# A plan of 2640 words in another order, and each attention's second result copy on ScalarE

## The chip, the cores and the metric

The kernel runs on one core of one Trainium2 chip. The metric is the device time of one execution in microseconds (us). The kernel before takes 887.47 us, the median of three runs (886.60, 887.47, 888.52).

The engines are called as the profile calls them: PE is TensorE, DVE is VectorE, ACT is ScalarE, POOL is GpSimd, and SP issues transfers. Each works through its own instructions in the order of the program and waits on semaphores for the results of the others.

## The reference

Sixteen batches of 256 tokens by 256 features, in float32, go through a cross attention with RMS norms (layer 0), and then through a block with a causal self attention (layer 1), a cross attention (layer 2) and a feed-forward part with 1024 hidden features. There are 16 heads of 16 features everywhere.

```python
# layer 0
q_norm, c_norm = rmsnorm(query, g_q), rmsnorm(context, g_c)
Q, K, V = heads(q_norm @ Wq), heads(c_norm @ Wk), heads(c_norm @ Wv)
attn = softmax(Q @ K.T * hd ** -0.5)             # the mask is all ones
x = rmsnorm(query + merge(attn @ V) @ Wo, g_out)
# layer 1: causal, queries and keys turned by their position (rope)
h = ln(x); x = x + attn_causal(rope(h @ wq), rope(h @ wk), h @ wv) @ wo
# layer 2: queries from x, keys and values from the context y, rope on both
h = ln(x); x = x + attn(rope(h @ wq), rope(y @ wk), y @ wv) @ wo
x = x + gelu(ln(x) @ fc1 + b1) @ fc2 + b2
```

## The kernel before, in words

**The work.** There are 48 attentions, one for each batch and layer. `ORDER` fixes which layer the i-th attention has (the string begins 000001010102); a batch's attention of layer 1 follows its layer 0, and layer 2 follows layer 1. After the 48 attentions the feed-forward parts of all batches run two batches at a time (`Mlp`); this last part, from about 680 us on, is written out as code and not touched by the plan but for its first steps.

**The plan.** Between a short head and that last part, all instructions come from the string `PLAN` (L54). Its words, such as `scores.6.1` or `take_last.5`, name a step and an attention. `step` (L1507) holds one Python generator per word: the first time a word appears it runs up to the first `yield`, the next time up to the second, and so on. So a word that stands four times has four parts, each issuing its instructions where the word stands. Since nothing reorders instructions later, the place of a word is its place in the queue of each engine that it uses, SP's and POOL's queues of transfers included. The words are grouped in the text by attention: a line begins with `scores.i.0`.

**The steps of one attention**, in the order in which one attention needs them:
- `stats`, `norm`: row statistics on DVE (L543), the inverse root on POOL (L525, L526), the normalized rows `xn` on DVE (L553). `keep` (L729, L620) then adds the output bias to the rows on POOL (L621, 128x512).
- `pieces`: DVE transposes 32x32 blocks into the tile `bits` (L584), and its second part sends it to DRAM (SP, L592). `pieces_in` fetches the turned rows `hT` (SP, L598). `turn` does the same through PE and ACT instead.
- `q`, `k`, `v`: a projection is 32 matmuls into one of three PSUM tiles `d` (L633 or L645). In layers 1 and 2, ACT adds the bias (L760) into a tile `a`; DVE turns by position (shuffle L768, two products L774, an addition L863, L866 or L810). The tag `a` has two buffers, and `bits` and `qa` use them too.
- `q_high`, `q_low`, `q_out`, `k_high`, `k_low`, `k_out` (layers 0 and 2, from the third attention on): a split in a high and a low part on ACT (L823, L875) and DVE (L830, L834, L879), and transfers on SP that put the parts on the rows where the matmuls need them (L840, L887). Layer 1 instead writes two masked copies of the query (L816 on DVE, L818 on ACT).
- `scores.i.n`: one block of scores, 16 matmuls (L953 in layer 1, L964 otherwise) into two PSUM tiles `S`, of which there are just two; then two exponentials on ACT (L976) into tiles `pt`. In layer 1, POOL clears what lies above the diagonal (L984).
- `values.i.n`: 8 matmuls for each block (L1007) into the PSUM tile `A`, of which there is one. After the first half of the features is done, the second part of `values.i.1` copies `A` to SBUF on ACT (`take(0, ...)`, L1022). After the second half, `take_last` (L1034) copies it; before, this copy is on DVE.
- `sums_in` (L1041) and `heads_in` (L1030): SP moves the softmax sums and the heads from the copied tile `av` to where they are needed. Both wait for the copies.
- `invert`: a reciprocal on DVE (L1051), out to DRAM and back over all rows (L1054, L1060). `divide`: a check sum on POOL (L1065), and the product on DVE (L1067).
- `project`: 32 matmuls (L645) and the addition to the rows on DVE (L1074 or L1080); `finish` (L1084) ends layer 0.

**Other words.** `load_piece`, `load_later` issue input and weight loads on POOL's queue, `load_early` and `load` on SP's. `send`, `receive` carry a row scale through DRAM. `combine` (L1480) does one of eight POOL operations (L1124, L1135) that prepare sums of the feed-forward weights; before, the first four calls prepare the second weight matrix and the last four the first one, whatever number the word has.

Of the kernel before, what the change touches and what calls it, by code (L numbers as in the profile page):

```python
# [54 lines left out]
scores.0.0 scores.0.0 v.0 scores.0.0 scores.0.1 q.1 scores.0.1 scores.0.1 spread.1 spread.1  # L55
scores.0.2 q.1 v.1 v.1 v.0 scores.0.2 v.0 scores.0.2 stats_x.3 values.0.0 values.0.1 stats_x.2
stats_x.3 scores.0.3 v.1 values.0.1 load_piece.5.0 k.1 stats_x.2 scores.0.3 send.2 stats_y.2
scores.0.3 k.2 send.2 k.1 load_piece.5.1
scores.1.0 load_early.4 k_high.2 load_early.0 k_low.2 q.2 scores.1.0 send.3 receive.2 scores.1.0
values.0.2 load_early.3 send.3 scores.1.1 q.3 scores.1.1 q.2 scores.1.1 values.0.3 k_out.2  # L60
q_high.2 scores.1.2 take_last.0 q_low.2 v.2 v.2 stats_y.2 scores.1.2 receive.3 q_low.2 stats_y.3
scores.1.2 q_out.2 values.1.0 stats_y.6 load_piece.6.1 scores.1.3 sums_in.0 stats_y.3 stats_x.6
k.3 scores.1.3 scores.1.3 load.4 values.1.1 k_high.3
scores.2.0 values.1.1 k_low.3 scores.2.0 values.1.2 q.3 invert.0 values.1.3 scores.2.0 heads_in.0
take_last.1 q_high.3 scores.2.1 invert.0 v.3 k_out.3 q_low.3 scores.2.1 q_low.3 heads_in.0
scores.2.1 v.2 stats_x.4 q_out.3 scores.2.2 k.4 stats_x.4 stats_y.4 sums_in.1 scores.2.2
load_piece.5.2 send.4 scores.2.2 values.2.0 v.3 send.4 divide.0 v.3 k_high.4 scores.2.3 q.4
load_early.2 scores.2.3 invert.0 invert.1 k_low.4 scores.2.3 divide.1 values.2.1 stats_y.4
receive.4 invert.1
scores.3.0 heads_in.1 values.2.1 stats_x.6 fold_of_att scores.3.0 heads_in.1 load_piece.5.3  # L70
values.2.2 divide.0 scores.3.0 q.4 values.2.3 k_out.4 q_high.4 scores.3.1 take_last.2 project.0
q_low.4 scores.3.1 invert.1 q_low.4 scores.3.1 values.3.0 q_out.4 project.0 fold_of_att scores.3.2
project.0 v.4 v.4 load_piece.6.0 scores.3.2 stats_y.8 project.0 scores.3.2 values.3.1 sums_in.2
finish.0 scores.3.3 values.3.1 stats.5 k.6 fold_of_att scores.3.3 v.4 stats.5 scores.3.3
values.3.2 load_later.0 norm.5 k_high.6 divide.1 load_piece.6.2
scores.4.0 heads_in.2 stats_x.8 values.3.3 scores.4.0 turn.5 send.6 send.6 take_last.3 scores.4.0
project.1 fold_of_att fold_of_att turn.5 heads_in.2 k_low.6 scores.4.1 invert.2 project.1 q.5
sums_in.3 scores.4.1 fold_of_att load_early.1 scores.4.1 receive.6 values.4.0 project.1 heads_in.3
q.5 scores.4.2 invert.3 k.5 project.1 invert.2 q.5 scores.4.2 q.5 load_later.1 invert.3 scores.4.2
q.5 values.4.1 load_piece.7.1 q.5 k.5 load_piece.7.0 scores.4.3 q.5 invert.2 values.4.1  # L80
load_piece.7.2 q.6 k.5 q.5 stats_y.6 k.5 scores.4.3 k.5 heads_in.3 v.5 v.5 scores.4.3 divide.2 k.5
load_piece.6.3 q.6 stats_x.8 values.4.2 invert.3 v.5 q_high.6
scores.5.0 divide.3 finish.1 q_low.6 k_out.6 values.4.3 scores.5.0 v.6 take_last.4 scores.5.0
scores.5.0 stats.7 sums_in.4 scores.5.1 divide.2 stats.7 q_low.6 project.2 v.6 scores.5.1 norm.7
scores.5.0 pieces.7 q_out.6 scores.5.1 scores.5.1 values.5.0 project.2 pieces.7 scores.5.2
project.2 scores.5.1 heads_in.4 k.8 send.8 invert.4 scores.5.2 project.2 divide.3 invert.4
scores.5.2 v.6 scores.5.2 values.5.1 finish.2 keep.5 k_high.8
scores.6.0 values.5.1 stats.9 pieces_in.7 project.3 scores.6.0 scores.5.2 k_low.8 stats.9
scores.6.0 values.5.2 heads_in.4 divide.4 norm.9 stats_y.8 project.3 scores.6.1 take_last.5
load_later.9 q.7 scores.6.1 project.3 sums_in.5 load_later.8 scores.6.1 pieces.9 heads_in.5  # L90
values.6.0 stats_y.10 q.7 scores.6.2 pieces.9 k.7 q.7 send.8 scores.6.2 invert.5 q.7 invert.5
scores.6.2 invert.4 q.7 values.6.1 q.7 scores.6.3 receive.8 q.7 k.7 q.8 invert.5 q.7 k.7
values.6.1 pieces_in.9 v.7 v.7 k.7 scores.6.3 load_later.4 k.7 load_piece.7.3 scores.6.3 k.7
heads_in.5 values.6.2 divide.5 q.8 project.3
scores.7.0 divide.4 q_high.8 v.7 k_out.8 project.4 scores.7.0 stats_x.10 scores.7.0 scores.7.0
values.6.3 heads_in.6 load_later.5 scores.7.1 divide.5 scores.7.0 take_last.6 project.5 project.4
scores.7.1 q_low.8 scores.7.1 scores.7.1 q_low.8 v.8 project.5 q_out.8 scores.7.1 stats.11
scores.7.2 sums_in.6 project.4 stats.11 q.9 scores.7.2 load_later.7 norm.11 scores.7.2 finish.3
scores.7.2 values.7.0 heads_in.6 pieces.11 stats_x.10 q.9 values.7.1
scores.8.0 load_piece.8.0 q.9 values.7.1 k.10 pieces.11 scores.7.2 scores.8.0 q.9 v.8 load_later.6  # L100
scores.8.0 send.10 values.7.2 v.8 send.10 stats_y.10 gain_ca k_high.10 q.9 scores.8.1 project.4
k.9 q.9 scores.8.1 keep.7 pieces_in.11 take_last.7 invert.6 scores.8.1 values.8.0 stats_x.14 k.9
invert.6 scores.8.2 q.9 v.9 v.9 k.9 load_piece.9.0 scores.8.2 k_low.10 divide.6 sums_in.7
load_piece.8.1 scores.8.2 k.9 values.8.1 keep.9 k.9 q.9 scores.8.3 values.8.1 invert.6 k.11 v.9
scores.8.3 k.9 heads_in.7 scores.8.3 finish.4 values.8.2 invert.7 receive.10 k.11 heads_in.7
scores.9.0 k.11 values.8.3 invert.7 scores.9.0 k.11 k_out.10 q.10 take_last.8 scores.9.0
scores.9.0 k.11 load_later.10 sums_in.8 scores.9.1 q.10 scores.9.0 stats.13 stats_x.14 q_high.10
v.10 divide.6 v.10 scores.9.1 divide.7 q_low.10 invert.7 stats.13 project.6 scores.9.1 q_low.10
scores.9.1 v.10 q_out.10 scores.9.2 project.6 scores.9.1 heads_in.8 invert.8 q.11 k.11 scores.9.2
load_piece.8.2 heads_in.8 divide.7 scores.9.2 load_piece.9.1 values.9.0 send.14 project.6  # L110
scores.9.2 q.11 invert.8 values.9.1 scores.9.2 k_high.11
scores.10.0 q.11 load_later.3 values.9.1 project.7 norm.13 scores.10.0 k_low.11 scores.10.0 q.11
values.9.2 k_out.11 pieces.13 q.11 scores.10.1 project.7 k.12 scores.10.1 take_last.9 q.11
scores.10.1 invert.8 values.10.0 stats.12 q_high.11 pieces.13 scores.10.2 stats.12 sums_in.9 v.11
q_low.11 scores.10.2 divide.8 norm.12 load_piece.10.0 k.12 heads_in.9 q_low.11 v.11 turn.12
scores.10.2 k.12 values.10.1 q_out.11 stats.16 turn.12 scores.10.3 pieces_in.13 values.10.1 v.11
fold_of_fc1 stats.16 scores.10.3 divide.8 q.12 load_later.2 k.12 scores.10.3 k.12 load_piece.8.3
k.12 values.10.2 q.12 stats_y.14
scores.11.0 fold_of_fc1 k_high.12 project.8 fold_of_fc1 invert.9 scores.11.0 stats_y.14 norm.16
heads_in.9 q.12 scores.11.0 project.6 values.10.3 k_low.12 invert.9 q.12 scores.11.1 q.12 k_out.12  # L120
k.13 scores.11.1 take_last.10 q.12 scores.11.1 heads_in.10 values.11.0 q_high.12 scores.11.2
invert.9 v.12 v.12 divide.9 q_low.12 scores.11.2 keep.11 send.14 q_low.12 scores.11.2 project.8
values.11.1 q_out.12 gain_fc1.0 k.13 scores.11.3 divide.9 k.14 sums_in.10 scores.11.3 v.12
scores.11.3 project.9 pieces.16 keep.12 values.11.1 k.13 k_high.14
scores.12.0 k.13 project.9 values.11.2 scores.12.0 k.13 pieces.16 values.11.3 heads_in.10 stats.15
scores.12.0 take_last.11 heads_in.11 stats.15 scores.12.1 k.13 q.13 receive.14 norm.15 scores.12.1
sums_in.11 invert.10 scores.12.1 k_low.14 divide.10 values.12.0 project.8 invert.10 q.13
scores.12.2 heads_in.11 q.13 values.12.1 scores.12.2 pieces_in.16 q.13 v.13 v.13 scores.12.2 q.13
q.13 values.12.1 invert.10 scores.12.3 q.13 q.13 pieces.15 q.14 scores.12.3 v.13 pieces.15
scores.12.3 k_out.14 values.12.2 q.14  # L130
scores.13.0 divide.10 fold_of_fc1 finish.6 k.15 scores.13.0 pieces_in.15 stats.19 scores.13.0
stats_x.17 scores.13.0 values.12.3 q_high.14 scores.13.1 take_last.12 k.15 invert.11 v.14 v.14
# [216 lines left out]
def xattn_kernel(  # L349
# [21 lines left out]
    nc = tc.nc  # L371
# [285 lines left out]
    class Att:  # L657
# [376 lines left out]
        def take_last(self, copy=nc.vector.tensor_copy):  # L1034

            self.take(1, copy)
# [459 lines left out]
    def begin(word):  # L1496
# [3 lines left out]
        if name == "combine":  # L1500
            return combine()
# [563 lines left out]
```

## Time and profile before

| | us |
|---|---|
| median of three runs | 887.47 |
| the profiled execution | 891.12 |
| its span | 889.40 |
| PE busy in the span | 871.22 |
| DVE, ACT, POOL busy | 690.87, 570.42, 349.33 |
| PE busy in 20 to 680 us (660 us) | 650.10 |
| copies L1022 on ACT | 49, median 0.587 |
| copies L1022 on DVE | 47, median 0.684 |

The profiled execution is one run with the hardware profiler on; its span reaches from the first to the last instruction. "Busy" is the time in which at least one instruction of that engine ran; the ends of matmuls are modelled, so a busy PE may still be slowed. A row of the windows view gives, for a stretch, the busy time (and instruction count) of PE, the weight loads PEld, DVE, ACT and POOL, then the granted clock of PE as a share of full speed, the share of the transfer engines, and GB/s. A row of the waits view gives who waited, for whom, how long in total, how often, and the longest. In a row of the timeline the two numbers are start and duration, `x2` merges equal neighbours, and the bracket gives the idle time before the first one and what ended it.

### The profile page before, as it was taken

What the parts mean: (1) busy time and instruction counts of PE and PEld (TensorE: products, weight loads), DVE (VectorE), ACT (ScalarE), POOL (GpSimd) and SP (SyncE); (2) the same over time, 40 slices, a digit from 0 to 9 for tenths busy, and PEclk for the clock granted to TensorE, in tenths of its full rate; (3) what the DMA queues carried; (4) which work ended last, traced back from release to release, by engine and by line L of the source; (5) the groups of instructions that cost most, each with busy time, mean ns of one, the idle gap of its engine ahead of it and who ended that gap; (6) DMA issues with size and microseconds to landing.
All of it is one profiled execution on the core that took longest, in us unless ns stands there. A gap on an engine that the chain in (4) does not pass through costs nothing.

```text
span 889.4 us, 32873 instructions
## 1 busy us (share of the span) xinstructions
PE 871.2 (98%) x13762; PEld 559.2 (63%) x13762; DVE 690.9 (78%) x1534; ACT 570.4 (64%) x801; POOL 349.3 (39%) x558
## 2 busy tenths in 40 slices
PE   8999999999999999999999999999999999999997
PEld 4455555555555555555554555555556799999997
DVE  5468789888888889889885888989894677777662
ACT  4787567776686767778756777777875733334440
POOL 3234766517364246175483335345142132221000
PEclk9999999999999999999999999999999999999999
DMA  8666455544444344343434233233431022111201
GB/s 273 208 193 176 147 163 175 178 132 133 134 148 123 110 134 161 117 159 120 155 118 145 84 124 111 87 118 116 158 107 54 17 72 72 57 44 44 72 25 50
DMA packets 101454, 107.04 MB, mean 120 GB/s; under 512 B 26602, under 2 KB 81778, under 8 KB 101298
## 3 DMA queue, kind: packets, MB, share of 16 engines
q1 hardware_dynamic: 96210, 89.89, 30.7%
q0 software_dynamic: 4400, 14.42, 5.7%
q8 instruction: 110, 1.80, 0.9%
q10 hardware_dynamic: 688, 0.54, 0.2%
q14 instruction: 46, 0.38, 0.1%
HBM read 46.33 MB, written 13.65 MB: 67 GB/s over the span
## 4 chain that ended last, share of the span: by engine, by line
PE 79%; DVE 8%; DMA 5%; ACT 2%; issue 2%; SPq 2%; POOL 2%; ACTq 0%; DVEq 0%; POOLq 0%
PE d L633 15%; PE d L645 14%; PE A L1007 14%; PE S L964 7%; PE upX L1221 6%; PE A L1319 6%; PE S L953 5%; PE downZ L1319 3%; PE upZ L1221 3%; PE d L1319 2%; PE d L1221 2%; ACT pt L976 1%; DMA turn_hop<-bits 1%; DMA qm<-qm 1%; DVE xn L553 1%
## 5 line engine op out<-in xcount | busy, mean ns | idle before, releaser
L976 ACT ACTIVATE pt<-S 128x1024 f32<-128x1024 f32 x224 | 217.7, 1023 | 98.9 <-PE S L953 59.4
L1007 PE MATMUL A<-pt,va 128*32 128x256 f32 (+1 forms) x3072 | 184.6, 363 | 2.9 <-ACT av L1022 2.7
L976 ACT ACTIVATE pt<-S,sy 128x1024 f32<-128x1024 f32 x128 | 136.4, 1115 | 35.5 <-PE S L964 26.2
L1007 PEld LDWEIGHTS A<-pt,va 128*32 128x32 f32 x3072 | 94.1, 110 | 68.0 <-issue 7.0
L984 POOL TENSOR_SCALAR_AFFINE_SELECT pt<-pt 128x512 f32<-128x512 f32 x128 | 90.7, 728 | 74.4 <-ACT pt L976 73.9
L964 PEld LDWEIGHTS S<-qm,kT 32*128 32x128 f32 x1920 | 66.9, 183 | 52.2 <-issue 24.2
L964 PE MATMUL S<-qm,kT 32*128 32x256 f32 x1920 | 93.5, 304 | 3.8 <-ACT pt L976 3.4
L621 POOL TENSOR_TENSOR cur<-cur,bias 128x512 f32<-128x512 f32 x48 | 64.8, 1353 | 32.9 <-DVE xn L553 32.7
L525 POOL TENSOR_SCALAR r_ln<-bmv 128x2 f32<-128x2 f32 x48 | 14.4, 300 | 149.6 <-DVE bmv L544 137.4
L953 PE MATMUL S<-qm,kT 32*64 32x512 f32 (+1 forms) x1152 | 63.3, 512 | 1.1 <-DVE kT L866 1.0
L760 ACT ACTIVATE a<-d,qk_bias 128x256 f32<-128x256 f32 x128 | 53.9, 477 | 14.0 <-PE d L633 4.8
L1243 ACT COPY g<-upX 128x512 f32<-128x512 f32 x28 | 15.0, 589 | 72.4 <-issue 68.1
L633 PE MATMUL d<-hT,sa 128*32 128x256 f32 x1024 | 61.4, 382 | 0.0
L553 DVE TENSOR_SCALAR xn<-cur,bmv,r_ln 128x256 f32<-128x256 f32 x96 | 47.5, 543 | 4.2 <-POOL r_ln L526 4.0
L1067 DVE TENSOR_TENSOR oT<-oT,inv 128x512 f32<-128x512 f32 x48 | 38.2, 798 | 15.1 <-DMA rq<-rq_hop 3.7
L774 DVE TENSOR_TENSOR a<-a,turn 128x512 f32<-128x512 f32 x64 | 47.9, 748 | 1.3
L1259 ACT ACTIVATE g<-g,fb 128x256 f32<-128x256 f32 x96 | 41.0, 499 | 11.1 <-DVE g L1248 11.1
L768 DVE STREAM_SHUFFLE u<-a 128x512 f32<-128x512 f32 x64 | 47.5, 743 | 0.4 <-issue 0.4
L774 DVE TENSOR_TENSOR u<-u,turn 128x512 f32<-128x512 f32 x64 | 47.0, 734 | 0.0
L1065 POOL TENSOR_TENSOR seen<-seen,sums 128x64 f32<-128x64 f32 x48 | 20.9, 436 | 62.9 <-DVE sums L1051 59.2
L633 PEld LDWEIGHTS d<-hT,sa 128*32 128x32 f32 x1024 | 30.3, 109 | 24.2 <-issue 3.2
L1022 DVE COPY av<-A 128x512 f32<-128x512 f32 x47 | 32.1, 683 | 13.4 <-PE A L1007 13.4
(176 smaller groups left out, 1701.1 us busy)
## 6 DMA issues: line engine op xcount, KB each, us to landing
kT<-hl SPq DMA_DIRECT2D x60, 256.0 KB
qm<-qm SPq DMA_DIRECT2D x60, 256.0 KB
oT<-av SPq DMA_DIRECT2D x192, 64.0 KB
inv<-inv_hop SPq DMA_DIRECT2D x96, 128.0 KB
turn_hop<-bits SPq DMA_DIRECT2D x33, 256.0 KB
hT<-turn_hop SPq DMA_DIRECT2D x92, 64.0 KB
out<-res SPq DMA_DIRECT2D x15, 256.0 KB
cur<-in_x POOLq DMA_DIRECT2D x11, 256.0 KB, 3.3
```

What stands on the lines that cost most here:

```text
L553: nc.vector.tensor_scalar(xn[:, c, :], src[:, c, :], mv[:, c, 0:1], r[:, c : c + 1], ALU.subtract, ALU.mult,)
L621: nc.gpsimd.tensor_tensor(t, t, bias_sb[:, row : row + D].unsqueeze(1).to_broadcast([P, NC, D]), ALU.add)
L633: nc.tensor.matmul(o, lhsT=w[:, k, at + t * P + j : at + t * P + j + 32], rhs=tokens, start=(k == 0), stop=(k == KC - 1), skip_group_check ...
L645: nc.tensor.matmul(ps[j : j + 32, c * D : (c + 1) * D], lhsT=some_tokens(src, k, c, j), rhs=w[:, k, at : at + D], start=(k == 0), stop=(k ...
L774: nc.vector.tensor_tensor(t, t, table.unsqueeze(1).to_broadcast([P, KC, S]), ALU.mult)
L953: nc.tensor.matmul(ps[64 * half : 64 * half + 64, 2 * m * u : 2 * m * (u + 1)] .rearrange("p (i s) -> p i s", i=2), lhsT=self.kT[r, t, at] ...
L964: nc.tensor.matmul(ps[:, at : at + m], lhsT=self.kd[r, i, t, kc * P : (kc + 1) * P].bitcast(F32R), rhs=self.qd[r, i, h, t, q0:S].bitcast(F ...
L976: nc.scalar.activation(pt[:, :, :w], ps[:, :, :w], AF.Exp, scale=scale)
L984: nc.gpsimd.affine_select(out=diag, in_=diag, compare_op=ALU.is_ge, fill=0.0, base=0, pattern=[[0, 2], [0, 2], [1, P]], channel_multiplier=-1,
L1007: nc.tensor.matmul(self.av[32 * r : 32 * r + 32, i, q0:S], lhsT=self.va[:, kc, 8 * t + 2 * r + i, :], rhs=pts[r // 2][:, r % 2, i * m : (i ...
L1221: nc.tensor.matmul(o if len(b.shape) == 2 else by_groups(o), lhsT=a[:, c * P : (c + 1) * P], rhs=b, start=(first and c % 2 == 0), stop=Tru ...
L1319: nc.tensor.matmul(ps[:, c, :], lhsT=a[f // 2][:, f % 2, c * P : (c + 1) * P], rhs=b[:, f, :], start=(first and c == 0 and f == 0), stop=True,
```

## The change

The plan's words are put in another order; the words, and how often each occurs, are the same, and `ORDER` stays. `take_last` copies with ACT where it copied with DVE; the 48th attention's, which is called after the plan, named ACT before. `combine` takes its word's number: 0 to 3 run the next operation for the second weight matrix, 4 to 7 the next for the first, in whatever order the words stand. Nearly every line of the plan differs; of the plan the diff below keeps attentions 6, 32, 45 and 46 whole and the first lines of 7.

```diff
-scores.6.0 values.5.1 stats.9 pieces_in.7 project.3 scores.6.0 scores.5.2 k_low.8 stats.9
-scores.6.0 values.5.2 heads_in.4 divide.4 norm.9 stats_y.8 project.3 scores.6.1 take_last.5
-load_later.9 q.7 scores.6.1 project.3 sums_in.5 load_later.8 scores.6.1 pieces.9 heads_in.5
-values.6.0 stats_y.10 q.7 scores.6.2 pieces.9 k.7 q.7 send.8 scores.6.2 invert.5 q.7 invert.5
-scores.6.2 invert.4 q.7 values.6.1 q.7 scores.6.3 receive.8 q.7 k.7 q.8 invert.5 q.7 k.7
-values.6.1 pieces_in.9 v.7 v.7 k.7 scores.6.3 load_later.4 k.7 load_piece.7.3 scores.6.3 k.7
-heads_in.5 values.6.2 divide.5 q.8 project.3
+scores.6.0 values.5.1 heads_in.4 project.3 load_later.6 stats.9 scores.6.0 load_piece.7.3 k_low.8
+scores.6.0 stats.9 values.5.2 invert.4 stats_y.10 load_later.4 invert.4 scores.6.1 load_later.9
+take_last.5 q.7 scores.6.1 norm.9 keep.5 pieces.9 scores.6.1 values.6.0 project.3 divide.4
+sums_in.5 q.7 scores.6.2 project.3 pieces.9 k.7 q.7 scores.6.2 heads_in.4 project.3 q.7 scores.6.2
+invert.4 values.6.1 q.7 q.7 scores.6.3 heads_in.5 q.7 v.7 k.7 invert.5 invert.5 divide.5
+scores.6.3 k.7 receive.8 v.7 load_piece.9.0 heads_in.5 q.8 q.7 k.7 stats_y.8 values.6.1 k.7
+scores.6.3 invert.5 values.6.2 k.7 divide.4 k_out.8
...
+scores.7.0 v.7 project.4 stats_x.10 scores.7.0 pieces_in.9 q.8 scores.7.0 scores.7.0 values.6.3
+project.4 q_high.8 load_piece.8.1 scores.7.1 divide.5 load_later.5 q_low.8 project.5 stats_x.10
+scores.7.1 q_low.8 take_last.6 q_out.8 scores.7.1 scores.7.1 v.8 project.5 sums_in.6 stats.11
...
-scores.32.0 invert.30 k.33 stats.37 divide.29 values.31.2 invert.30 scores.32.0 norm.35 keep.33
-k.33 send.36 v.33 scores.32.0 k.33 combine.0 take_last.31 scores.32.1 invert.30 norm.37
-load_piece.14.3 q.33 scores.32.1 pieces.35 v.33 divide.30 stats.39 k.33 sums_in.31 scores.32.1
-values.32.0 k.33 combine.2 pieces.35 scores.32.2 q.33 heads_in.30 project.29 keep.37 scores.32.2
-q.33 v.33 scores.32.2 values.32.1 norm.39 invert.31 pieces.37 scores.32.3 invert.31 divide.31
-load_piece.15.2 heads_in.31 q.34 q.33 scores.32.3 divide.30 heads_in.31 q.33 scores.32.3
-project.30 q.33 values.32.1 pieces_in.35 q.33 q.33 project.29 values.32.2 project.30
+scores.32.0 values.31.1 k.33 load_piece.14.3 heads_in.30 values.31.2 divide.29 scores.32.0
+combine.0 k.33 pieces.35 v.33 scores.32.0 take_last.31 receive.34 divide.30 send.36 stats.39
+sums_in.31 scores.32.1 k.33 stats.39 q.33 invert.30 scores.32.1 v.33 norm.39 scores.32.1
+values.32.0 k.33 send.36 q.33 scores.32.2 k.33 pieces_in.35 project.29 v.33 scores.32.2 q.33
+scores.32.2 divide.30 values.32.1 heads_in.31 invert.31 scores.32.3 q.33 divide.31 values.32.1
+invert.31 q.34 q.33 scores.32.3 q.33 scores.32.3 q.33 project.30 q.34 q.33 project.29 q_high.34
+values.32.2 pieces.39
...
-scores.45.0 k_high.46 q.46 values.44.3 heads_in.43 scores.45.0 k_low.46 project.42 scores.45.0
-q.46 k_out.46 take_last.44 scores.45.1 q.46 sums_in.44 v.46 v.46 q.46 keep.44 scores.45.1
-project.42 heads_in.44 scores.45.1 divide.43 values.45.0 stats.47 q_high.46 heads_in.44
-scores.45.2 invert.44 values.45.1 stats.47 q_low.46 scores.45.2 invert.44 k.47 q_low.46
-scores.45.2 norm.47 q_out.46 mlp.0.stats values.45.1 keep.47 turn.47 k.47 invert.44 scores.45.3
-turn.47 keep.46 v.46 values.45.2 scores.45.3 k.47 q.47 divide.44 k.47 scores.45.3 mlp.0.stats k.47
-k.47
-scores.46.0 q.47 divide.44 values.45.3 scores.46.0 q.47 project.44 scores.46.0 q.47 q.47 k_high.47
-scores.46.1 q.47 v.47 v.47 take_last.45 scores.46.1 k_low.47 sums_in.45 scores.46.1 mlp.1.stats
-values.46.0 q_high.47 scores.46.2 k_out.47 project.43 q_low.47 scores.46.2 q_low.47 scores.46.2
-mlp.0.norm values.46.1 q_out.47 scores.46.3 invert.45 project.44 invert.45 divide.45 scores.46.3
-mlp.0.keep v.47 mlp.0.turn project.43 heads_in.45 values.46.1 scores.46.3 mlp.0.turn values.46.2
-mlp.1.stats
+scores.45.0 invert.43 q.46 k_low.46 values.44.3 scores.45.0 q.46 project.42 take_last.44
+scores.45.0 q.46 sums_in.44 q.46 scores.45.1 q.46 v.46 v.46 divide.43 k_out.46 scores.45.1
+divide.43 keep.44 project.42 scores.45.1 heads_in.44 values.45.0 stats.47 keep.46 q_high.46
+values.45.1 invert.44 stats.47 scores.45.2 q_low.46 invert.44 k.47 q_low.46 scores.45.2 norm.47
+q_out.46 scores.45.2 v.46 keep.47 turn.47 heads_in.44 mlp.0.stats k.47 scores.45.3 keep.43 turn.47
+invert.44 q.47 scores.45.3 k.47 mlp.0.stats scores.45.3 k.47 values.45.1 k.47
+scores.46.0 q.47 k.47 values.45.2 divide.44 scores.46.0 q.47 values.45.3 scores.46.0 divide.44
+q.47 k_high.47 scores.46.1 take_last.45 project.44 q.47 scores.46.1 sums_in.45 q.47 scores.46.1
+k_low.47 values.46.0 q_high.47 k_out.47 scores.46.2 v.47 v.47 q_low.47 scores.46.2 q_low.47
+scores.46.2 mlp.0.norm q_out.47 values.46.1 scores.46.3 project.44 mlp.0.keep project.43 invert.45
+scores.46.3 invert.45 values.46.1 scores.46.3 mlp.0.turn project.43 heads_in.45 keep.45
+values.46.2 v.47 heads_in.45 mlp.0.turn
...
-        def take_last(self, copy=nc.vector.tensor_copy):
+        def take_last(self, copy=nc.scalar.copy):
...
-    def combine():
+    def combine(n):
         if not mixed:
...
-            combined.extend([*[combine_down()] * 4, *[combine_up()] * 4])
-        next(combined.pop(0))
+            combined.extend([combine_down(), combine_up()])
+        next(combined[n // 4])
...
-            return combine()
+            return combine(int(args[0]))
```

## The prediction

> **What bounds the kernel now.** I read the page's busy shares first, then the two stretches of the windows view, then the list of waits, and last the timeline of the worst place.
>
> ```profile
> span 889.4 us, 32873 instructions
> PE 871.2 (98%) x13762; PEld 559.2 (63%) x13762; DVE 690.9 (78%) x1534; ACT 570.4 (64%) x801; POOL 349.3 (39%) x558
> ...
> 20.00:680.00 660.00, 650.10 (x12070) 363.87 (x12064) 542.98 (x1204) 479.63 (x611) 311.38 (x493) 1.00 0.43 138
> 460.00:480.00 20.00, 17.90 (x296) 9.35 (x292) 14.41 (x27) 10.53 (x14) 8.10 (x12) 0.91 0.37 116
> ```
>
> TensorE bounds it. From 20 to 680 us, which is the stretch that the plan orders, PE is busy 650.1 of 660 us, so only 9.9 us of idle time can be won there. Neither the work of PE nor the last 209 us change. In that stretch DVE is busy 543 us (82%) and ACT 479.6 us (73%). The idle time lies in few places; 460 to 480 us alone holds 2.1 us, and there the granted clock is 0.91 instead of 1.00. The waits and the timeline say what made them:
>
> ```profile
> PE S L964 <- ACT pt L976: 3.4, 5, 1.5
> PE A L1007 <- ACT av L1022: 2.7, 3, 1.2
> ```
>
> ```profile
> 464.54 1.73 POOL L621 TENSOR_TENSOR cur<-cur,bias 128x512 f32<-128x512 f32 x1
> 465.16 1.66 DVE L866 TENSOR_TENSOR kT<-a,u 128x512 f32<-128x512 f32 x1
> 466.93 0.84 ACT L760 ACTIVATE a<-d,qk_bias 128x256 f32<-128x256 f32 x2 [3.48 <-DVE kT L866]
> 467.66 2.12 ACT L976 ACTIVATE pt<-S,sy 128x1024 f32<-128x1024 f32 x2
> 468.83 0.38 PE L964 MATMUL S<-qm,kT 32*128 32x256 f32 x2 [1.48 <-ACT pt L976]
> 470.67 3.39 PE L633 MATMUL d<-xT,w 128*32 128x256 f32 x32
> ```
>
> This is the whole mechanism in six lines. A POOL addition (L621, a `keep`) runs beside a DVE addition, which takes 1.66 us where its median is 0.69; ACT waits 3.48 us in its queue for the DVE result, two exponentials start late, PE waits 1.48 us (and 0.62 us more on the second half), and the next 32 matmuls take 3.39 us where the same line takes 1.86 us elsewhere, because the clock had fallen. The place costs 1.48 + 0.62 + 1.53 = 3.6 us. So a good order keeps POOL's long additions away from DVE's chains and keeps ACT's queue free of operations that wait.
>
> **Part 1: the last copy moves from DVE to ACT.** 47 copies are moved (the 48th is on ACT already, after the plan).
>
> ```profile
> L1022 ACT COPY av<-A x49: 578/587/616, 22.0 to 683.6; 128x512 f32<-128x512 f32 x49
> L1022 DVE COPY av<-A x47: 626/684/692, 34.2 to 670.6; 128x512 f32<-128x512 f32 x47
> ```
>
> DVE loses 47 x 0.683 = 32.1 us of work and the 13.4 us that it stood idle for these copies; ACT gains 47 x 0.587 = 27.6 us. In the stretch DVE falls to 511 us (77%) and ACT rises to 507 us (77%). None of this is PE's time, so the direct gain is 0, and what counts is who waits. Behind a moved copy, ACT's next operation in the new plan is an exponential in 37 of 47 cases; PE needs both exponentials of a block before it may write the next scores, for there are just two such tiles. On the copy itself wait the next attention's first value matmul (the result has one tile) and the SP queue: before, SP's `sums_in` waited 35.4 us in 18 cases for DVE's copy, with `heads_in`, `q_out` and `k_out` transfers queued behind it. The plan places the copy as before (1.3 us of matmuls behind its producer on average, 1.45 before), so SP's wait I cost at 0.
>
> ACT's idle time in the stretch falls from 180 to 153 us. PE's idle waits for ACT (3.4 + 2.7 = 6.1 us) scaled by 180/153 give a loss of **1.1 us**. The bounds: below, -3 us (a gain), if ACT's 0.59 for DVE's 0.68 frees the one result tile sooner wherever PE waited for it; above, +10 us, worked out as a rival. I take 1.1 as nearest to the rows of PE's own waits.
>
> A rule to weigh: the DVE copies run 626 to 692 ns, even the 25 that overlap a POOL tensor operation (L526, L621, L1124, L1135; 682 ns on average), while the two-input DVE addition of L866 ranges from 622 to 1657 ns. [...]
>
> **Part 2: the new order.** Both plans hold the same 2640 words, each as often, so no instruction is added or dropped. The pieces of `combine` become free in their order (two generators instead of one list); they are the same eight POOL operations of about 1.3 us, at cost 0. What moves are distances, and I lay both plans out with durations of the trace (a projection 1.73 us from x64 in 3.59 less x32 in 1.86; a block of scores 0.48 or 0.96 and of values 0.86, by the starts of successive matmuls), as PE work between two words.
>
> - *POOL beside DVE.* Before, attention 32 holds `keep.33`, `combine.0`, `combine.2` and `keep.37` within some 7 us of PE work, which is the place above. In the new plan it holds `combine.0` alone; `keep.33` goes 28 us later, `keep.37` 71 us, `combine.2` 18 us. Of the 3.6 us I take 3.0 as gained. Two more places have the same cause: near 215 us and 555 us a project waits 0.70 and 0.58 us for a DVE product (L1067) that took 1.72 and 1.16 us beside POOL work. I take half, 0.6. In return attentions 45 and 46 get two more `keep`s (`keep.43`, `keep.45`), 2.7 us of POOL work, right where PE idles 2.4 us in 660 to 680 us.
> - *DVE's load.* DVE work over PE work for two neighbouring attentions peaks at 1.14 (45 and 46) before and 1.00 after, the copies included; for ACT the peak goes from 1.07 to 1.11 (43 and 44). So at the end DVE is relieved and POOL is loaded: of the 2.4 us I take 0.6 as gained.
> - *The `bits` tiles.* A `pieces` transfer out must have read its tile before the second next projection may use that buffer. At 110 us ACT waits 3.96 us for such a transfer (5.04 us from issue to landing) and PE then 1.16 + 0.75 us. The PE work between the two grows from 5.62 to 7.29 us on average, the least from 2.68 to 3.99, here from 3.07 to 4.80 (the projection of `v.7` comes between). But the value matmul that waited has the same 6.53 us of PE work ahead of it in both, so I take 0.8 of 1.9 us.
> - *Other chains.* From `invert`'s transfer to `divide` 6.23 us become 5.91, from `divide` to `project` 2.47 become 2.82, from `pieces_in` to its first projection 11.5 become 13.1, from the last query or key step to the scores 3.22 become 3.62, though `scores.7.0` now follows `k.7` with nothing between (0.86 before). Sum 0. Input loads (POOL's and SP's queues): the nearest to its reader is `load_piece.6.1`, 6.1 us ahead, where POOL's loads land in 3.3 to 4.4 us; cost 0, and about 1 us if one is late.
> - *New accidents.* 2640 words in another order make places that this trace can't show. I price them at 1 us: the mean size of the places of before, 9.9 us over some ten.
>
> A second rule, for the size of such a place: here the clock fell after waits of 1.48 and 0.62 us, and 32 matmuls then took 1.53 us longer. [...]
>
> **The sum.** Gained 3.0 + 0.6 + 0.6 + 0.8 = 5.0 us; lost 1.1 (ACT) + 1.0 (accidents) = 2.1 us; net 2.9. The profiled execution took 891.12 us, 1.7 beyond its span of 889.40, and would take 888.2. It lies 3.65 us (0.4%) above the median of the three runs, 887.47; the same 2.9 us from there give **884.5 us**, 0.33% faster. A measurement of this kernel can tell about 0.2%, 1.8 us, from no change, so below 885.7 counts as faster and above 889.3 as slower.
>
> **Rivals.**
> 1. *ACT's queue takes over* (slower). Each moved copy stands ahead of an exponential and may first wait for its matmuls, as DVE's did (13.4/47 = 0.29 us). In 37 cases exponentials come 0.59 + 0.29 = 0.87 us later, 32 us in all. It decides where PE already arrives before the exponentials: PE's weight loads for scores waited for ACT in 44 + 11 of 176 blocks, 31%, so 10 us reach PE. In place of the 1.1 us: 884.5 - 1.1 + 10 = **893**. For it: 117 waits of ACT for scores show that the two are coupled closely. Against it: ACT keeps 153 us of idle time, and 20 of 49 copies on ACT waited 15.6 us already while PE idled 2.7 us for them.
> 2. *As much given back as gained* (no change). The new order has its own meetings of POOL and DVE and its own late transfers, about the 5 us of before: **887.5**. For it: most of the mean distances differ by little.
> 3. *Nearly all idle time goes*: 9.9 us of idle and 1.5 of slow clock, less the 1.1: about **877** to 879. For it: DVE's relief of 32 us covers every chain. Against it: late transfers (5.04 us where neighbours take 2.0 to 2.8) are in no order's hand.
>
> That the change doesn't do what it says I exclude: no word passes a copy to `take_last`, so the new default moves all 47.
>
> **Chances.** The forecast (881 to 885.7) 0.42, rival 3 0.13, rival 2 0.18, rival 1 and its smaller forms (889.3 to 897) 0.27. Faster 0.55, same 0.18, slower 0.27. The likeliest case's own range is 881 to 886; the range that should hold 8 times in 10 reaches to rival 3 and into rival 1: 877 to 893.
>
> **What would show it.** Right: 47 + 49 copies of L1022 on ACT at 0.59 us and none on DVE; PE idle between 20 and 680 us about 7 us; no row of PE's waits over 1 us near attention 32 and the clock at 1.00 there; DVE near 511 us in the stretch. Wrong: PE's waits for ACT (pt and av) well above 6.1 us would be rival 1; a new DVE row of 1.5 us beside L621 with a PE wait behind it, above all near 660 us, would be rival 2; a transfer out of `bits` that ACT waits for, the fourth step.

## The result and the profile after

The new kernel takes **880.01 us** (median of 4 runs, 879.68 to 880.08) where the kernel before takes 888.0 beside it (886.60 to 890.05): ratio 0.9911, 95% interval 0.9889 to 0.9934. Run once more in another series, it took 879.98 us (7 runs) beside 886.37 (18 runs), ratio 0.9931 [0.9906, 0.9956]. So it is 6 to 8 us faster, where 2.9 us were forecast; the direction held and so did the wide range (877 to 893), the size did not: 880.01 lies below the forecast's own 881 to 885.7 and above the third rival's 877 to 879, where the prediction had put no chance. The profiled execution took 880.08 us, 1.7 beyond its span of 878.4.

The engine row of the page:

```profile
PE 867.9 (99%) x13762; PEld 558.9 (64%) x13762; DVE 660.0 (75%) x1487; ACT 593.4 (68%) x848; POOL 352.9 (40%) x558
```

Three rows of the windows view; the columns are the window, its length, the busy time and count of PE, PEld, DVE, ACT and POOL, PE's granted clock, the DMA engines' busy share and GB/s:

```profile
20.00:680.00 660.00, 656.74 (x12170) 370.89 (x12163) 514.26 (x1155) 509.50 (x667) 317.34 (x497) 1.00 0.43 139
460.00:480.00 20.00, 20.00 (x384) 10.79 (x380) 14.03 (x26) 13.20 (x18) 11.19 (x16) 1.00 0.40 133
660.00:680.00 20.00, 18.86 (x216) 12.43 (x217) 8.42 (x18) 11.60 (x16) 3.79 (x6) 1.00 0.16 50
```

In the stretch that the plan orders, PE is now busy 656.74 of 660 us; of 9.9 us of idle time 3.3 are left. DVE and ACT have the load that was worked out (514 and 510 us, for 511 and 507). From 460 to 480 us PE never stops and the clock is full. The waits of PE, in total us, times and longest, say the same:

```profile
PE idle L1522 <- POOL zeros L466: 2.1, 1, 2.1
PE S L966 <- ACT pt L978: 1.3, 3, 0.6
PE d L635 <- DMA hT<-turn_hop: 0.4, 1, 0.4
PE d L635 <- DVE va L921: 0.4, 1, 0.4
PE d L570 <- DVE xn L555: 0.4, 2, 0.2
PE d L647 <- DVE oT L1069: 0.3, 1, 0.3
```

The first row is the start of the span, ahead of the plan. Behind it no wait is longer than 0.6 us, and PE no longer waits for `av` at all (2.7 us before). Of the groups of instructions, the copy off PSUM is one row now, with 96 copies on ACT; what they cost ACT beside their 590 ns is 20.4 us of waiting for PE (15.6 before):

```profile
L1024 ACT COPY av<-A 128x512 f32<-128x512 f32 x96 | 56.6, 590 | 20.6 <-PE A L1009 20.4
```

### The profile page after: what moved, and what is told of

It reads as the page before. It is cut to its first block, busy times and chain, and to the rows that moved or that the text cites. A ratio compares the mean times of both kernels' runs of the same rounds, so it can differ in the third digit from the quotient of the medians.

```text
span 878.4 us, 32887 instructions
## 1 busy us (share of the span) xinstructions
PE 867.9 (99%) x13762; PEld 558.9 (64%) x13762; DVE 660.0 (75%) x1487; ACT 593.4 (68%) x848; POOL 352.9 (40%) x558
## 4 chain that ended last, share of the span: by engine, by line
PE 86%; DVE 4%; DMA 3%; issue 2%; SPq 2%; ACT 2%; POOL 1%; ACTq 0%; DVEq 0%; POOLq 0%
PE d L647 17%; PE d L635 16%; PE A L1009 15%; PE S L966 8%; PE upX L1223 6%; PE S L955 6%; PE A L1321 6%; PE downZ L1321 3%; PE upZ L1223 3%; PE d L1321 2%; PE d L1223 2%; ACT pt L978 1%; PE d L570 1%; PE downX L1321 1%; DMA hT<-turn_hop 1%
## 5 line engine op out<-in xcount | busy, mean ns | idle before, releaser
L986 POOL TENSOR_SCALAR_AFFINE_SELECT pt<-pt 128x512 f32<-128x512 f32 x128 | 94.4, 757 | 77.3 <-ACT pt L978 76.7
L966 PE MATMUL S<-qm,kT 32*128 32x256 f32 x1920 | 92.6, 303 | 1.5 <-ACT pt L978 1.3
L527 POOL TENSOR_SCALAR r_ln<-bmv 128x2 f32<-128x2 f32 x48 | 15.6, 325 | 138.5 <-DVE bmv L546 137.4
L1024 ACT COPY av<-A 128x512 f32<-128x512 f32 x96 | 56.6, 590 | 20.6 <-PE A L1009 20.4
L762 ACT ACTIVATE a<-d,qk_bias 128x256 f32<-128x256 f32 x128 | 53.9, 477 | 4.6 <-PE d L635 4.4
L1069 DVE TENSOR_TENSOR oT<-oT,inv 128x512 f32<-128x512 f32 x48 | 35.9, 749 | 11.3 <-issue 5.5
L1067 POOL TENSOR_TENSOR seen<-seen,sums 128x64 f32<-128x64 f32 x48 | 19.4, 404 | 57.2 <-DVE sums L1053 50.6
```

The source lines that it names most:

```text
L966: nc.tensor.matmul(ps[:, at : at + m], lhsT=self.kd[r, i, t, kc * P : (kc + 1) * P].bitcast(F32R), rhs=self.qd[r, i, h, t, q0:S].bitcast(F ...
L986: nc.gpsimd.affine_select(out=diag, in_=diag, compare_op=ALU.is_ge, fill=0.0, base=0, pattern=[[0, 2], [0, 2], [1, P]], channel_multiplier=-1,
L1024: copy(av, self.av)
```

## The experiments

Two theories were open. **The copy**: DVE is relieved of 32 us of work, and that covers the chains PE waited for. **The order**: the distances between the words do it. Within the order, the prediction had one large term, POOL's additions beside DVE in attention 32.

**One part alone.** The old order with the copy on ACT (`e1_copy_alone`), and the new order with the copy on DVE (`e2_order_alone`); either is this one line in the one kernel or the other:

```
-        def take_last(self, copy=nc.vector.tensor_copy):
+        def take_last(self, copy=nc.scalar.copy):
```

> The old order with the copy on ScalarE alone. The order theory (the gain is the spacing of POOL's additions, DVE's chains and transfers in the plan): within 2 us of the kernel before, most likely 1 us slower, with PE's idle waits for ACT between 6 and 9 us where they were 6.1, and the place at attention 32 still there with 2 us or more of PE idle time. The copy theory (32 us less DVE work ends the stalls by itself): 4 to 8 us faster, PE idle in 20 to 680 us falling from 9.9 to below 6 us.

> The new order with the copy left on DVE. The order theory: 5 to 8 us faster than the kernel before, that is within 2 us of the changed kernel, PE idle between 20 and 660 us below 5 us, DVE 32 us busier. The copy theory: at most 3 us faster, with new waits of PE behind DVE's queue, since the order was laid out for a DVE without these copies.

Measured: the copy alone 890.5 us, ratio 1.0037 [1.0015, 1.0059], so 3.3 us *slower*, more than the 2 us at most that the order theory allowed; the order alone 881.2, ratio 0.9933 [0.9912, 0.9955], 5.9 us faster. The copy theory falls. In the old order the copies cost 3.3 us, and not the 10 of the first rival. PE's waits for `pt` rise from 3.4 us to this row of the copy alone,

```profile
PE S L964 <- ACT pt L976: 5.0, 7, 2.3
```

and the longest, 2.3 us, is the place in attention 32 again. But PE's idle time in this profile, 9.6 us of 20 to 680 us, is no more than in the two profiles of the kernel before (9.9 and 9.3), which lie over 3 us above that kernel's median: with the copies, the usual run looks like a long run of the kernel before. The granted clocks say the same. They are 0.997 or less in 9 of the 12 runs, as in both of those profiles, which have the place; of all 82 runs of the kernel before in the three series it is so in 20. So the copies seem to make that place frequent; that this comes by ACT's queue, as the first rival had it, is not shown. In the new order the same copies cost nothing that can be measured (ratio 0.9933 without them, 0.9911 and 0.9931 with them).

**POOL beside DVE.** Three of POOL's additions leave attention 32 in the old order (`e3_pool_spread`), and three go back into it in the new one (`e5_pool_back`):

```
e3, old order: keep.33 -> before scores.34.1; keep.37 -> before scores.38.1; combine.2 -> before scores.33.2
e5, new order: keep.33 -> behind k.33; combine.2 -> before send.36; keep.39 -> before scores.32.2
```

> The old order, copy on DVE, with three words alone moved out of attention 32 to the attentions where the new plan has them: keep.33 to 34, keep.37 to 38, combine.2 to 33. The POOL theory of that place (POOL's additions stretch DVE's): 2 to 3.6 us faster, the clock 1.00 in 460 to 480 us, no DVE row of L866 above 1.2 us there. The rival (the place comes from ACT's and DVE's load alone): within 1 us of the kernel before, the waits of 1.5 and 0.6 us still there.

> The new kernel with three of POOL's additions put back into attention 32 (keep.33, combine.2 and keep.39), so that it holds four again, as in the old order. Theory of the contention (the term of 3.0 us): a DVE addition beside them takes over 1.1 us, ACT waits in its queue for it, a wait of PE over 1 us for pt comes back between 450 and 465 us, and the time is 882 to 884 us. Theory of the room (an addition is harmless where the chains of DVE and ACT have time to spare, and the new order gives them that): DVE's additions are stretched all the same, but no PE wait over 0.3 us stands there, and the time is within 1 us of the new kernel's 880.0.

Measured: 886.68 us for the first, ratio 1.000 [0.9975, 1.0024]; 880.45 for the second, ratio 0.9926 [0.9904, 0.9948], like the new kernel itself. Neither moves the time, where the contention theory had 2 to 3.6 us less for the first and 882 to 884 us for the second. The first did what it should in its trace, where the wait at 467 us fell from 1.48 and 0.62 us to one of 0.37 (the second profile below shows that this may be chance); the second brings the stretched addition back. Its timeline, start and duration in us, with the idle time before in brackets:

```profile
455.97 0.84 ACT L762 ACTIVATE a<-d,qk_bias 128x256 f32<-128x256 f32 x2
456.67 1.66 POOL L623 TENSOR_TENSOR cur<-cur,bias 128x512 f32<-128x512 f32 x1 [0.56 <-DVE xn L555]
457.30 1.58 DVE L868 TENSOR_TENSOR kT<-a,u 128x512 f32<-128x512 f32 x1
457.35 2.12 ACT L978 ACTIVATE pt<-S,sy 128x1024 f32<-128x1024 f32 x2 [0.53 <-PE S L966]
```

The addition for `kT` takes 1.58 us beside POOL's, as long as the 1.66 of before, where the median is 0.69; but here ACT's bias step (L762) ran ahead of it without a wait, and the exponentials behind start as soon as their scores are there. So the stretch is real and here harmless: what hurt, by these traces, was that the old order had an ACT instruction at the head of its queue that needed the late result (L760, 3.48 us of waiting).

**The kernel before once more** (`e11_before_again`), for a second profile, since its first execution lay 3.65 us above the median.

> The kernel before once more, for a second profile of it. If the place near 467 us (PE waits of 1.48 and 0.62 us and a lower clock) belongs to the order, it stands in this execution too. If it belongs to the one execution that was profiled, 3.65 us above its median, it is smaller or gone here, and the time is near 887 us; the waits at 110, 215, 372 and 666 us stay.

It took 889.81 us, and the place stood there again: 1.19 and 0.62 us, with the clock at 0.91 in 460 to 480 us.

```profile
461.96 1.26 POOL L1124 TENSOR_TENSOR down_t<-fc,down_t 128x512 f32<-128x512 f32 x1
462.56 1.14 DVE L553 TENSOR_SCALAR xn<-cur,bmv,r_ln 128x256 f32<-128x256 f32 x2
463.78 1.28 POOL L621 TENSOR_TENSOR cur<-cur,bias 128x512 f32<-128x512 f32 x1 [0.56 <-DVE xn L553]
464.31 1.30 DVE L774 TENSOR_TENSOR u<-u,turn 128x512 f32<-128x512 f32 x1
465.64 0.69 DVE L866 TENSOR_TENSOR kT<-a,u 128x512 f32<-128x512 f32 x1
466.45 0.84 ACT L760 ACTIVATE a<-d,qk_bias 128x256 f32<-128x256 f32 x2 [3.75 <-DVE kT L866]
468.35 0.38 PE L964 MATMUL S<-qm,kT 32*128 32x256 f32 x2 [1.19 <-ACT pt L976]
```

Here the addition for `kT` itself takes its usual 0.69 us. What runs longer beside POOL's additions is the work ahead of it on DVE: the rows `xn` (L553) take 1.14 us where they take 0.72 at 468 us, and the product L774 1.30 where it takes 0.65 at 470 us. The waits at 110, 372 and 666 us stay, as expected; that at 215 us does not. So the place at 467 us belongs to the order, but not to every execution: the runs of before spread from 883.3 to 891.9 us in that series, and of four more traces with the old words there, two show it (the copy alone, and `e7` below) and two do not (`e6` and `e10` below; in both PE had waited 1.4 to 1.8 us for a transfer's sake near 387 us). The new kernel spreads from 879.2 to 881.8, 2.6 us where under 2 were expected.

**The old and the new order joined** at the third block of attention 18, where they differ by four words; the copy on DVE (`e7_new_then_old`, `e8_old_then_new`). An earlier try joined them at attention 24, where they differ by eleven words (`e4_old_then_new`, copy on ACT).

```
e7: the new plan up to scores.18.2, then the words left in the old plan's order
e8: the old plan up to scores.18.2, then the words left in the new plan's order
e4: the old plan up to scores.24.0, then the words left in the new plan's order
```

> The old order up to the beginning of attention 24, then what is left in the new order; the copy on ScalarE throughout. By the trace of before, 3.3 of the 9.9 us of PE idle time in 20 to 680 us and none of the slow clock lie ahead of attention 24. So where the gain is the sum of the places that the trace shows, 5 to 6 us of the 8 us are gained here. If the gain is spread evenly over the plan: 4 us. If the places before attention 24 hold most of it: below 3 us.

> The new order up to the third block of attention 18 (about 262 us), then the old one; the last copy on DVE throughout, so that it stands between the kernel before and the run with the order alone (5.7 us apart). At this joint the two orders differ by four words. Theory that the gain is spread over some ten places: the part is worth what the traces show up to 262 us, 4.2 us of idle time before and 2.0 with the new order, so 2.2 us: ratio 0.9975. Rival, one place decides: 1.000 or 0.9935.

> The complement: the old order up to the third block of attention 18, then the new one; last copy on DVE. Spread: after 262 us the idle time is 6.6 us before and 2.8 with the new order, 3.8 us less, of which 2.1 are the place at 467 us that not every run has, so 2 to 4 us: ratio 0.9955 to 0.998, and both parts together give the 5.7 us. Rival, one place decides: 1.000 or 0.9935. A joint that stalls by itself would show as one long PE wait at 255 to 275 us.

Measured: 885.2 us, ratio 0.9977 [0.9959, 0.9994], and 885.13, ratio 0.9983 [0.9967, 0.9999]: about 2 us for each part, 4 of the 5.9 together, which the intervals allow to be all. Neither interval reaches 1.000 or 0.9935, so no single place decides: the gain is spread over both parts. The join at attention 24 made a stall of its own (2.82 us at 350 us), came out at 888.51, ratio 1.0015 [0.9991, 1.004], and tells nothing.

**The place at 110 us, twice.** First one word in the old order, the projection of `v.7` ahead of the second step of `k.7`; then three weight loads on POOL's queue moved away from it.

```
e6:
-receive.8 q.7 k.7 q.8 invert.5 q.7 k.7 values.6.1 pieces_in.9 v.7 v.7 k.7
+receive.8 q.7 v.7 k.7 q.8 invert.5 q.7 k.7 values.6.1 pieces_in.9 v.7 k.7
e10: load_later.4 -> before scores.8.1; load_later.9 -> before scores.9.2; load_later.8 -> before scores.10.0
```

> The old order with one word moved: the first step of v.7 stands ahead of the second step of k.7, as in the new order. Theory that the order makes the place at 110 us: both PE waits there (1.16 and 0.75 us) go, and the time is 1.5 to 1.9 us under the kernel before (ratio 0.998). Theory that the late transfer makes it, whatever stands between (the step of the prediction): 0.8 us or nothing, and a wait over 0.5 us remains between 108 and 115 us.

> The old order with three weight loads of 256 KB on POOL's queue (load_later.9, load_later.8, load_later.4) moved from 101 to 104 us to between 120 and 155 us. Theory of the loads: the transfer out of bits at 104.7 us lands late (5.0 us) because the 16 DMA engines are full with loads issued in the 3 us before it (1.03 busy, 285 GB/s in 104 to 106 us); without them it lands in under 3.5 us, ACT waits under 2 us for it, the PE waits of 1.16 and 0.75 us at 110 us shrink by at least 1.2 us, and the time is 1.2 to 1.9 us under the kernel before, if no other hop meets the loads. Rival (the prediction: late transfers are in no order's hand): it still takes about 5 us, and the time is that of the kernel before.

Measured: 887.54 us, ratio 1.0005 [0.9986, 1.0024], and 887.74, ratio 1.0004 [0.9981, 1.0027]. Neither gains, for two reasons. The word left the place as it was (waits of 0.94 and 0.76 us). The loads did what their theory said, and then something else was late. The timeline of the kernel before, second profile:

```profile
101.39 1.54 POOL L1437 DMA_DIRECT2D fc<-in_fc  x2
102.40 0.77 DVE L584 STREAM_TRANSPOSE bits<-xn 128x256 f32<-128x256 f32 x2
103.00 0.72 POOL L1437 DMA_DIRECT2D fc<-in_fc  x1
103.12 1.16 SPq L1030 DMA_DIRECT2D oT<-av  x2
104.38 0.52 SPq L592 DMA_DIRECT2D turn_hop<-bits  x1
109.44 0.84 ACT L760 ACTIVATE a<-d,qk_bias 128x256 f32<-128x256 f32 x2 [3.75 <-DMA turn_hop<-bits]
```

and of the same stretch with the loads moved:

```profile
102.31 0.77 DVE L584 STREAM_TRANSPOSE bits<-xn 128x256 f32<-128x256 f32 x2
104.28 0.52 SPq L592 DMA_DIRECT2D turn_hop<-bits  x1
106.58 0.84 ACT L760 ACTIVATE a<-d,qk_bias 128x256 f32<-128x256 f32 x2 [0.98 <-DMA turn_hop<-bits]
112.78 0.69 DVE L794 TENSOR_TENSOR qa<-d,rq 128x512 f32<-128x512 f32 x1 [2.46 <-DMA rq<-rq_hop]
113.39 0.68 DVE L1067 TENSOR_TENSOR oT<-oT,inv 128x512 f32<-128x512 f32 x1
114.13 3.62 PE L645 MATMUL d<-w0o,oT 128*32 128x256 f32 x32 [1.85 <-DVE oT L1067]
```

From issue to landing the transfer out of `bits` takes 5.1 us with the loads and 2.3 without. In 104 to 106 us the DMA engines' busy share is 0.99 with them and 0.58 without. ACT's wait falls from 3.75 to 0.98 us, and both PE waits at 110 us go. But now DVE comes early to L794, which needs another transfer, `rq`, and waits 2.46 us with L1067 behind it in the queue; PE waits 1.85 us for that, and the 32 matmuls after it take 3.62 us instead of 1.93, since the clock falls (0.72 in 112 to 118 us). The old stall had hidden this one; why `rq` is late was not tried. In the new kernel both are gone:

```profile
101.79 0.77 DVE L586 STREAM_TRANSPOSE bits<-xn 128x256 f32<-128x256 f32 x2
102.59 0.34 SPq L594 DMA_DIRECT2D turn_hop<-bits  x1
105.11 0.84 ACT L762 ACTIVATE a<-d,qk_bias 128x256 f32<-128x256 f32 x2
```

SP issues the transfer right behind the transpose (nothing of `oT<-av` stands ahead of it), POOL issued the last of its loads at 98.4 to 99.9 us, some 3 us ahead of it, and ACT doesn't wait. Measured is 5.1 us against 2.3 for one and the same transfer, with the three loads just ahead of it and without them; how the DMA engines share their time between the queues no run here shows.

**One more word moved.** Every kernel so far keeps two waits of 0.60 and 0.54 us near 664 us. The new kernel with one word moved (`e9_up2_later`), and the new kernel itself beside it (`e12_new_again`):

```
-scores.47.1 mlp.1.stats sums_in.46 mlp.0.up2 scores.47.1 heads_in.46 scores.47.1 divide.45
+scores.47.1 mlp.1.stats sums_in.46 scores.47.1 heads_in.46 scores.47.1 mlp.0.up2 divide.45
```

> The new kernel with one word moved: the MLP step mlp.0.up2, whose two copies of 0.59 us on ACT stand ahead of the exponentials of scores.47.1, goes behind them. Theory: the two waits of PE near 664 us (0.60 and 0.54 us, for pt), which every version so far keeps, come from these copies: they go, and the time is 1.0 us under the new kernel's. Rival: the exponentials are late for the value matmuls or the result copy instead; both waits stay in some form and the time is the same within 0.3 us.

> The new kernel once more, beside the others, as the yardstick for the run with mlp.0.up2 moved and for the spread of its times: 879.7 to 880.5 us, spread under 2 us where the kernel before spreads over 9 us.

Measured: 878.2 us (6 runs, 877.21 to 881.0), ratio to the kernel before 0.992 [0.9893, 0.9948]; the new kernel 879.98, ratio 0.9931 [0.9906, 0.9956]. The medians are 1.8 us apart, and 4 of the 6 runs lie under every run of the new kernel; but the ranges and the intervals overlap, so a gain over the new kernel is likely and not shown by the times. The trace shows that the two waits are gone. Of PE's waits for `pt` this is left:

```profile
PE S L966 <- ACT pt L978: 0.2, 1, 0.2
```

and the windows view of the last 20 us of attention:

```profile
660.00:680.00 20.00, 20.00 (x217) 13.61 (x212) 10.79 (x23) 13.09 (x19) 3.37 (x5) 1.00 0.15 46
```

PE is busy in all 20 us, for 18.86. The two waits that came from two copies of 0.59 us at the wrong place of ACT's queue had added up to 1.1 us.

## Why the prediction was right in sign and small in size

PE's idle time in gaps above 100 ns, in us, by place, in five traces; the first three are of the old order (single gaps of 0.3 us and less are left out, and one of 0.58 at 555 us that only the first has):

| us | before | before again | additions spread | new | new again |
|---|---|---|---|---|---|
| 110 to 121 | 1.91 | 1.70 | 1.63 | 0.45 | 0 |
| 213 to 253 | 0.93 | 0.86 | 0.70 | 0.26 | 0 |
| 372 to 376 | 0.81 | 1.23 | 1.31 | 0 | 0 |
| 443 to 470 | 2.55 | 2.70 | 0.59 | 0 | 0 |
| 662 to 667, `A` | 1.06 | 1.05 | 1.05 | 0 | 0 |
| last 15 us | 1.32 | 1.32 | 1.32 | 1.32 | 1.32 |
| 152 (new) | 0 | 0 | 0 | 0.41 | 1.18 |
| 505 to 646 (new) | 0 | 0 | 0 | 0.61 | 0.62 |

1. *POOL beside DVE, 3.0 us gained.* DVE's work does run longer beside POOL's additions (in the first profile of before, the four additions for `kT` that overlap such work of POOL take 1.16 us on average, the other twelve 0.70) and ACT does wait for it (3.48 and 3.75 us), but the stretched instruction differs from execution to execution (in the second profile it is not the addition for `kT`), and the size came from one execution. The place stands in some executions of the old order, with 1.8 to 2.9 us of waits and the slow clock behind, and not in others; the run with the additions spread, whose trace lacks it, has the median of before (interval -2.2 to +2.1 us). The 20 runs of before with a granted clock of 0.997 or less average 889.5 us, the other 62 886.0. If those 20 are the ones with the place, it is worth 3.5 us in a quarter of the executions, so by this estimate about 0.8 us where 3.0 were taken, too little for that run to tell. I had taken the sum from the profiled execution and carried the 2.9 us over to the median, though it lay 3.65 us above that.
2. *Two project waits, 0.6.* Neither project wait is in the second profile; in place of the one at 215 us it has a wait of 0.60 us for exponentials at 220 us, so something of 0.7 to 0.9 us between 213 and 253 us stands in all three traces of the old order, but not always the same wait. The cause was read too narrowly as well: both products (L1067) had first waited 1.36 and 1.20 us for a transfer (`inv`), and most of the one at 214 us ran ahead of POOL's addition, which began at 215.11 us.
3. *The end, 0.6 of 2.4.* Mis-sized: the wait for `av` of 1.05 us stands in all traces with the old end and in none with the new. The other 1.3 us stay.
4. *The `bits` tiles, 0.8 of 1.9.* The step that failed. I had written that late transfers "are in no order's hand" and held this against the third rival. The run with the loads moved shows that this lateness is the order's own making: it comes from the loads that POOL issues just ahead (5.1 us with them, 2.3 without). In the new kernel 1.5 to 1.9 us go. My reason from the plan, that a projection comes between, is refuted by the run with that word alone.
5. *Other chains, sum 0.* Also wrong. I compared mean distances in PE work; the waits at 372 us (0.8 to 1.3 us, most of it a project) went as well. DVE and ACT together stand idle for transfers 27.0 and 25.8 us in the two profiles of before (20 to 680 us; rows of their waits that a DMA ended), 26 to 34 in the other kernels with the old order throughout, 33, 18 and 23 in the three joined ones (`e4`, `e7`, `e8`), and 12 to 19 in all with the new one. That goes with the times in the main, but not throughout (`e7` with 18 us takes 885.2 us, the new kernel with 18 takes 880.0), and only the place at 110 us was tried by itself, so the rest of this cause is inferred.
6. *ACT's queue, 1.1 lost.* In the old order the copies cost 3.3 us; in the new order, nothing that can be measured. I had scaled the waits of one trace, but the price depends on the order.
7. *New accidents, 1.0 lost.* Somewhat low: the two rows marked new hold 1.0 and 1.8 us.

With the places as the traces show them, the sum would be 1.6 (110 us) + 0.7 (213 to 253) + 1.1 (372) + 1.05 (the end) - 1.4 (new places) = 3.0 us, and some 3.6 more in the executions that have the place at 467 us: 3 to 7 us for the 6 to 8 measured. Both profiles of before are of executions over 3 us above its median, so its places may be somewhat large here. The gaps above 100 ns don't hold all of it. The trace with the additions spread has 7.6 us of them and the new one 3.2, 4.4 apart, while their spans (885.4 and 878.4) are 7.0 apart; the smaller gaps hold next to nothing of the other 2.6 us (they sum to 0.5 and 0.3 us). Some 2.4 us of it lie in PE's busy time, 870.2 against 867.9 us for the same 13762 matmuls, above all in the value matmuls (169.0 against 167.1 us) and a score form (93.8 against 92.6). The ends of matmuls are modelled, so short waits may hide there; this part stays open. So the 9.9 us of idle time were not all that an order can win, as the prediction had it. The third rival was right in direction, for another reason than it gave: not DVE's relief, since the order alone brings most of it.

## What to carry to other kernels

A wait that is removed by itself may only uncover the next late thing in the same queue, so a sum over the waits of a kernel that is tight can overstate single repairs, as it did twice here, and understate an order that moves them all. Before a place of one profile gets a price, see whether it stands in a second profile, and whether the profiled execution lies at the median. When a transfer is late, look at what the other queues issued just ahead of it, which is in the order's hand: here three loads of 256 KB, issued in the 3 us before, went with 5.1 us for a transfer that took 2.3 without them.

## What the runs showed of the hardware

In these traces no one length of a wait goes with a fall of the clock. Single waits of PE of 1.67 us (`e7`, at 153 us) and 1.76 us (`e6`, at 386 us) left the next 32 matmuls at full speed (1.93 us; the clock 1.00 in 150 to 160 us of the one and in 385 to 392 of the other). One of 1.85 us did not (`e10`, 3.62 us), and neither did 1.48 and 0.62 us with two matmuls between (the kernel before, 3.39 us) nor 1.19 and 0.62 us (its second profile), both with the clock at 0.91 over 20 us. But 1.16 and 0.75 us with 16 matmuls between, at 110 us of the kernel before, left it full again (1.93).

The clock record of a trace says where the clock changed. In the profile of the kernel before it is full from 20 to 680 us but for 470.25 to 473.67 us, 3.41 us at half speed (0.50), and the four entries of the record begin 136, 1 and 121 times 3.41 us apart. In the new kernel's it is full all through this stretch, and its two entries begin 255 times 3.41 us apart. If 20 to 680 us of the kernel before are cut into pieces of 3.41 us that begin where the slow one does, PE stands idle for 2.10 us in the piece just ahead of the slow one and for 1.16 at most in any other; the two waits at 110 us fall into two pieces (1.16 and 0.76 us).

Half of 3.41 us is 0.09 of 20 us and 0.28 of 6, so one such slow piece accounts for the mean clocks of four more profiles: 0.91 in 460 to 480 us of the second profile, of the copy alone and of `e7`, and 0.72 in 112 to 118 us of `e10`. PE's waits just ahead add up to 1.81 (1.19 and 0.62), 2.91 (2.29 and 0.62), 1.83 (1.21 and 0.62) and 1.85 us. So where the clock fell, PE had waited 1.81 us or more, while single waits of 1.67 and 1.76 us left it full, and so did the 1.91 us in two waits at 110 us, which the pieces take apart. What the clock goes by, these rows don't show.
